# A two-layer attention kernel: where a half projection, a value piece, the first loads and the last denominators stand

## The chip, the cores and the metric

The kernel runs on one core of a Trainium2 chip. The metric is device time in microseconds (us). Before the change three runs took 3836.77, 3838.15 and 3838.79 us, so the median is 3838.15.

A core has a matrix engine (TensorE, PE in the profile; its weight loads are PEld), a vector engine (VectorE, DVE), an engine for functions such as exp (ScalarE, ACT), a general one (GpSimd, POOL) and SyncE (SP), which here only issues transfers (DMAs). TensorE writes its products to an accumulator memory, PSUM. Here PSUM is used as eight buffers of 128 x 512 floats, called banks.

## The reference

Sixteen images of 256 channels and 32 x 32 = 1024 positions pass through two layers, all in float32:

```python
# layer 0: 4 heads of 64
q, k, v = split(x @ w_proj + b_proj)             # per head
attn = softmax(q @ k.T * 64 ** -0.5)
x = (attn @ v) @ w_out + b_out + x
# layer 1: 8 heads of 32
g = group_norm(x)                                # 32 groups of 8 channels
q, k, v = split(g @ qkv_w.T)
attn = softmax(q @ k.T * 32 ** -0.5 + phys_bias) # one number per head
x = x + (attn @ v) @ proj_w.T + proj_b
h = group_norm(x)
x = x + gelu(h @ w1.T + b1) @ w2.T + b2          # 1024 hidden units
```

A softmax divides by the sum of its exponentials, the denominators below. A group norm needs mean and variance over all positions of a group, so it can start only when all of x is there.

## The kernel before, in words

**Layout.** Channels lie on the 128 partitions in two chunks (`CC = 2`), positions along the rows. Positions are handled in two halves of 512 (`NT = 2`, `TB = 512`); keys in eight blocks of 128 (`SB = 8`).

**PSUM.** `wide` (L218) gives one of three double buffers of two banks each, `s0` to `s2`, the least recently used first; a number in the set `kept` is passed over. `bank` (L224) gives one of two single banks, `b0` and `b1`. That makes all eight.

**Products by columns.** `product` (L243, the matmuls of L246) cuts a product into pieces of `cols[0]` columns: 32 inside the attentions, 128 elsewhere. A float32 matmul stands in the trace as two records.

**First attention** (`attention_a`, L289). It works through four items, a half of the positions and a chunk of two heads each, with eight key blocks per item. One step, called a unit here, multiplies the scores `s_a` (L303), lets ScalarE take their exponentials `e_a` (L311), and two units later multiplies them with v into `acc_a` (L324), while VectorE adds the exponentials up in `es_a` (L336). Even items gather in banks 0 and 1, odd ones in double buffer 2, which is in `kept` meanwhile and leaves it when the item ends (L343). Then ScalarE copies one half out (L340) and VectorE adds the other (L341).

**Denominators.** When both chunks of a half are done, `normalise` (L348) multiplies the sums with ones (`den_a`, L355). `denominators` (L258) writes the result to memory in another shape, inverts it there as 128 x 16 (L267), adds it to the totals `dsum` and `isum`, from which the kernel decides at its end whether all sums were in range, and reads it back spread over the partitions (L273). `scale` (L368) multiplies by it, and `project` calls `out_proj` (L520, tile `o`), whose result VectorE adds to x (L533) with statistics for the norm (L537).

**Second attention** (`attention_b`, L398). A unit takes two key blocks for four heads: scores `s_b` (L422) in banks 0 and 1 and all three double buffers, exponentials `e_b` (L437), sums `es_b` (L452), `acc_b` in bank 0 (L461), denominators `den_b` in bank 1 (L485), projection `j`.

**Norms.** `group_norm` (L540) averages over channel groups by two small matmuls (`gm`, `gv`) with short VectorE steps between, and writes the normed tile (L595) that the next products read.

**The order of work.** Functions are put off by counts of steps: `later.after(n, fn)` runs `fn` at the n-th following `tick`. `run` (L750) goes through an attention's units, runs the pieces that `fill` lists for a unit and ticks. Pieces are the projections for q, k and v (`qkv`, L603: pieces `qk` and `v`), and the two products of the MLP (`mlp`, L703: `hidden` at L709 and `outputs`, both tile `m`). Image b's second attention is filled with its own remaining `qk` and `v` pieces, image b-1's `outputs` and image b+1's first projections. The `hidden` pieces of b-1 stand between b's two attentions, while b's first norm is computed. The library's scheduler then orders each engine's instructions from this written order: it may issue ahead one that is ready sooner by its own estimate. `keep_in_program_order` pins one instruction behind the one written before it on its engine, not the later ones behind it. Engines meet through semaphores, and each engine runs its queue in order.

**The ends.** Weights `wp` are loaded on ScalarE's and GpSimd's queues (L92), biases on GpSimd's (L104 to L110), the other weights on ScalarE's (L125), x on SP's (L235). The exponential of `phys_bias` is taken at L157. In the last image four of the eight `outputs` pieces are kept back for the end (L821), where the last norm and the last MLP have nothing else beside them.

Of the kernel before, what the change touches and what calls it, by code (L numbers as in the profile page):

```python
# [54 lines left out]
def kernel(  # L55
# [44 lines left out]
    bp = b_proj.rearrange("(g i t d) -> i t d g", i=2, t=3, d=D0)  # L100
    bqk = const.tile([P, 3, HEADS0 // 2], F32, name="bqk")
    for i in range(2):
        for t in range(3):
            nc.gpsimd.dma_start(bqk[i * D0 : (i + 1) * D0, t, :], bp[i, t])  # L104
    pb = const.tile([P, HEADS1], F32, name="pb")
    nc.gpsimd.dma_start(pb, phys_bias.partition_broadcast(P))
# [15 lines left out]
    def load_mat(w, name):  # L122
        k, n = w.shape
        t = const.tile([P, k // P, n], F32, name=name)
        nc.scalar.dma_start(t, w.rearrange("(c p) n -> p c n", p=P))  # L125
        return t

    wo = load_mat(w_out, "wo")
# [5 lines left out]
    ident = const.tile([P, P], F32, name="ident")  # L134
    make_identity(nc, ident)
# [14 lines left out]
    mhalf = const.tile([P, CC], F32, name="mhalf")  # L150
    nc.gpsimd.memset(mhalf, -0.5)
    ones = const.tile([P, D0], F32, name="ones")
    nc.gpsimd.memset(ones, 1.0)
# [3 lines left out]
    nc.scalar.activation(ebias, pb, AF.Exp)  # L157
    eones = const.tile([P, HEADS1, D1], F32, name="eones")
    nc.vector.tensor_copy(eones, ebias.unsqueeze(2).to_broadcast([P, HEADS1, D1]))
# [4 lines left out]
    with ExitStack() as first:  # L164
        first_pass(
            first, tc, x, out,
            dict(
                wp=wp, bqk=bqk, pb=pb, bo=bo, g1w=g1w, g1b=g1b, g2w=g2w,
                g2b=g2b, pjb=pjb, m1b=m1b, m2b=m2b, wo=wo, wq=wq, wpj=wpj, w1=w1,
                w2=w2, ident=ident, gavg=gavg, mhalf=mhalf, ones=ones, eones=eones,  # L170
                bvo=bvo,
                in_range=in_range,
            ),
        )
# [14 lines left out]
def first_pass(ctx, tc, x, out, k):  # L189
# [23 lines left out]

    def use(n):
        order.remove(n)
        order.append(n)
# [10 lines left out]

    dsum, isum = (act.tile([P, 4 * TB // P], F32, name=n) for n in ("dsum", "isum"))
# [3 lines left out]
    def load_x(b):  # L232
        t = act.tile([P, CC, S], F32, tag="x", name=f"x_{b}", bufs=3)
        for cc in range(CC):
            nc.sync.dma_start(t[:, cc, :], x[b, cc * P : (cc + 1) * P, :])  # L235
        return t

# [51 lines left out]
    def attention_a(b, qT, kT, v, project):  # L289
# [24 lines left out]
        def weigh(i, kb, e):  # L314
            t, c = items[i]
            if kb == 0:
                if i % 2:
                    acc = wide(f"acc_{key}_{i}", 2)
                    accs[i] = [acc[:, h, :] for h in range(2)]
                else:  # L320
                    accs[i] = [bank(f"acc_{key}_{i}_{h}", h) for h in range(2)]
            for h in range(2):
                for g in range(2):
                    nc.tensor.matmul(  # L324
                        accs[i][h][g * D : (g + 1) * D, :],
                        v[h * HALF : (h + 1) * HALF, kb, c * 2 + g],
                        e[h * HALF : (h + 1) * HALF, g, :],
                        start=(kb == 0),
                        stop=(kb == SB - 1),
                    )  # L330
            if kb == 0:
                held[i] = e
                return
            if kb == 1:
                sums[i] = work.tile([P, 2, TB], F32, tag="es", name=f"es_{key}_{i}", bufs=4)
            nc.vector.tensor_add(sums[i], held[i] if kb == 1 else sums[i], e)  # L336
            if kb == SB - 1:
                r = res[:, c, t * TB : (t + 1) * TB]
                one, two = accs.pop(i)
                nc.scalar.copy(r, one)  # L340
                nc.vector.tensor_add(r, r, two)  # L341
                if i % 2:
                    kept.discard(2)  # L343
                if c == CC - 1:
                    later.after(1, lambda: normalise(t))
# [21 lines left out]

        def scale(t, full):  # L368
            r = res[:, :, t * TB : (t + 1) * TB]
            halves = [  # L370
                y.rearrange(form, c=CC, h=2)
                for y, form in ((r, "p c (h q) -> p c h q"), (full, "p (h c q) -> p c h q"))
            ]
            tc.keep_in_program_order(nc.vector.tensor_mul(halves[0], *halves))
            later.after(1 if t < NT - 1 else 4, lambda: project(t, res))
# [10 lines left out]
        while pending:  # L386
            weigh(*pending.pop(0))
            if not pending:
                cols[0] = P
            yield  # L390
# [7 lines left out]
    def attention_b(b, qT, kT, v, project):  # L398
# [82 lines left out]
        def normalise(i, r, last):  # L481
            t, c = items[i]
            den = bank(f"den_{key}_{i}", 1)
            for g in range(G):
# [6 lines left out]
                )  # L491
            denominators(
                f"{key}_{i}", den_copy(f"{key}_{i}", den), TB,
                ((3, 5) if b + 1 < B else (1, 1)) if last else (1, 1),
# [3 lines left out]
        def scale(i, r, last, full):  # L498
            t, c = items[i]
            tc.keep_in_program_order(nc.vector.tensor_mul(r, r, full))  # L500
            if c == CC - 1:
                wait = (10 if b + 1 < B else 1) if last else 1
                later.after(wait, lambda: project(t, res[t]))
# [16 lines left out]
    def out_proj(key, w, nk, src, bias, xs, t, stats):  # L520
        ps = wide(f"{key}_{t}")
        for co in range(CC):
            for kc in range(nk):
                product(
                    ps[:, co, :],
                    w[:, kc, co * P : (co + 1) * P],
                    src(kc),
                    start=(kc == 0),
                    stop=(kc == nk - 1),
                )  # L530
        for co in range(CC):
            y = xs[:, co, t * TB : (t + 1) * TB]
            nc.vector.scalar_tensor_tensor(  # L533
                y, ps[:, co, :], bias[:, co : co + 1], y, ALU.add, ALU.add
            )
            if stats is not None:
                nc.vector.bn_stats(stats[:, co, t, :], y)  # L537


    def group_norm(key, src, stats, gw, gb, tag, out_tile, wait):  # L540
# [25 lines left out]
        def variances():  # L566
# [3 lines left out]

            dv = small.tile([P, CC], F32, tag="dv", name=f"dv_{key}")
# [7 lines left out]
        def apply():  # L579
            rstd = small.tile([P, CC], F32, tag="rstd", name=f"rstd_{key}")  # L580
            for sl, ps in averages(f"gv_{key}", st["tv"]):
                nc.vector.tensor_scalar(rstd[sl], ps, EPS, None, ALU.add)
            nc.gpsimd.tensor_tensor(rstd, rstd, k["mhalf"], ALU.pow)
# [19 lines left out]
    def qkv(key, D, src, weights, b_qk, v_scale, qT, kT, v_dst):  # L603
        def qk(ch, which, t):
            ps = wide(f"qk_{key}_{ch}_{which}_{t}")[:, 0]
# [16 lines left out]
        def v(n):  # L622
            ps = wide(f"v_{key}_{n}")[:, 0]
# [47 lines left out]
    def attention_0(b, qkv_tiles, xb, norm):  # L671
# [3 lines left out]
        def project(t, res):  # L675
            out_proj(
                f"o{b}", k["wo"], CC,
                lambda kc: res[:, kc, t * TB : (t + 1) * TB],
                k["bvo"], xb, t, stats,
            )  # L680
            if t == NT - 1:
                norm(stats)
# [3 lines left out]
    def attention_1(b, qkv_tiles, xb, norm):  # L686
# [3 lines left out]
        def project(t, res):  # L690
            out_proj(
                f"j{b}", k["wpj"], CC,
                lambda kc: res[:, kc, :],
                k["pjb"], xb, t, stats,
            )
            if t == NT - 1:
                norm(stats)
# [70 lines left out]


    xs = {0: load_x(0)}  # L770
    tiles0, (first_qk, first_v) = qkv_0(0, xs[0])
    run_pieces(first_qk + first_v)

# [17 lines left out]
    for b in range(B):  # L791
# [20 lines left out]

        run_pieces(qk[:n] + v[:1])
        own = [v[1], qk[n], v[2], qk[n + 1], v[3], *qk[n + 2 :]]
# [4 lines left out]
        if b == B - 1:  # L819

            now, end = outputs[:4], outputs[4:]  # L821
# [9 lines left out]
        for m, pieces in enumerate(rest):  # L831
# [7 lines left out]
                    4 if b + 1 < B else 2,  # L839
# [308 lines left out]
```

## Time and profile before

| | us |
|---|---|
| median of 3 runs | 3838.15 |
| the profiled execution | 3836.97 |
| its span, first to last instruction | 3835.1 |
| outside the span | 1.9 |
| TensorE busy | 3783.2 |
| VectorE busy | 2214.2 |
| ScalarE busy | 2033.7 |

A line of a waits view names the waiting engine, tile and line, then what it waited for, the total in us, the number of times and the longest. A timeline line has the start and the time taken in us, engine, line, operation, output tile <- inputs, shape (for TensorE first rows * columns of the array, then the moving operand) and the count merged into it; in brackets the idle time before it and who ended it. Matmuls overlap: one that takes 0.59 us is followed by the next of its kind before it ends, so starts are compared, not ends. Times in all views run from the start of the span.

### The profile page before, as it was taken

To read this page: it belongs to the slowest core of one execution; us is meant where nothing else is said; L and a number is where in the kernel's file an instruction comes from. 1 tells how busy PE (TensorE), PEld (TensorE's weight loads), DVE (VectorE), ACT (ScalarE), POOL (GpSimd) and SP (SyncE) were. 2 spreads that over 40 slices of the span, in tenths; PEclk is the share of its full clock that TensorE was granted. 3 is DMA by queue.
4 is the path that set the end of the run, shared out by engine and by line. 5 is a ranking of instruction groups with operands and counts; after the bars stand their busy time and mean duration, and the time that the engine had idled before them with its cause. 6 is when DMAs were issued, how large, how long until landed. Compare 5 with 4: busy or idle time off the path is not lost.

```text
span 3835.1 us, 87391 instructions
## 1 busy us (share of the span) xinstructions
PE 3783.2 (99%) x38637; PEld 1508.9 (39%) x38637; DVE 2214.2 (58%) x2761; ACT 2033.7 (53%) x2625; POOL 86.1 (2%) x252
## 2 busy tenths in 40 slices
PE   9999999999999999999999999999999999999999
PEld 3333343333433334333343333433333333343435
DVE  4574646646466464665656556565564655646572
ACT  4555546555455554555545455554655546555461
POOL 1000000000000000000000000000000000000000
PEclk9999999999999999999999999999999999999999
DMA  2000000000000000010000001010000000000000
GB/s 83 10 16 12 30 12 16 27 13 30 12 16 28 11 30 12 19 29 7 30 12 27 21 10 32 7 32 15 13 30 7 32 15 13 29 7 24 12 14 23
DMA packets 62450, 78.58 MB, mean 20 GB/s; under 512 B 35344, under 2 KB 36880, under 8 KB 62064
## 3 DMA queue, kind: packets, MB, share of 16 engines
q1 hardware_dynamic: 57728, 68.72, 5.9%
q8 instruction: 304, 4.98, 0.5%
q10 hardware_dynamic: 3712, 3.80, 0.3%
q14 instruction: 82, 0.67, 0.1%
q0 software_dynamic: 624, 0.41, 0.1%
HBM read 54.54 MB, written 17.56 MB: 19 GB/s over the span
## 4 chain that ended last, share of the span: by engine, by line
PE 90%; DVE 5%; issue 2%; ACT 2%; DMA 1%; POOL 0%; SPq 0%; ACTq 0%; POOLq 0%; DVEq 0%
PE s_b L422 12%; PE m L709 12%; PE acc_b L461 12%; PE m L246 11%; PE s_a L303 10%; PE acc_a L324 9%; PE qk_b L246 6%; PE qk_a L246 6%; PE v_b L246 3%; PE j L246 3%; PE v_a L246 3%; DVE es_a L336 2%; PE o L246 2%; PE den_b L485 1%; ACT e_a L311 1%
## 5 line engine op out<-in xcount | busy, mean ns | idle before, releaser
L437 ACT ACTIVATE e_b<-s_b 128x1024 f32<-128x1024 f32 (+1 forms) x1280 | 982.7, 864 | 469.4 <-PE s_b L422 469.4
L452 DVE TENSOR_TENSOR es_b<-es_b,e_b 128x1024 f32<-128x1024 f32 x768 | 900.0, 1220 | 361.1 <-ACT e_b L437 361.1
L311 ACT ACTIVATE e_a<-s_a 128x1024 f32<-128x1024 f32 x512 | 521.4, 1025 | 450.1 <-PE s_a L303 438.3
L303 PE MATMUL s_a<-q,k 64*64 64x512 f32 x4096 | 562.1, 593 | 2.4 <-DVE x L533 2.4
L324 PE MATMUL acc_a<-e_a,v 64*64 64x512 f32 x4096 | 555.1, 589 | 0.0
L422 PE MATMUL s_b<-q,k 32*64 32x512 f32 x8192 | 536.3, 601 | 5.8 <-DVE res_b L477 4.9
L336 DVE TENSOR_TENSOR es_a<-es_a,e_a 128x1024 f32<-128x1024 f32 x384 | 469.0, 1221 | 111.5 <-ACT e_a L311 106.7
L461 PE MATMUL acc_b<-e_b,v 128*32 128x512 f32 x4096 | 492.1, 598 | 0.0
L709 PE MATMUL m<-gn_h,w 128*128 128x512 f32 x1024 | 460.8, 601 | 6.0 <-DVE mean_g L569 3.8
L246 PE MATMUL m<-g,w 128*32 128x256 f32 (+1 forms) x7616 | 464.0, 379 | 0.0
L246 PEld LDWEIGHTS m<-g,w 128*32 128x32 f32 (+1 forms) x7616 | 277.7, 112 | 215.8 <-issue 41.5
L717 ACT ACTIVATE g<-m,m1b 128x512 f32<-128x512 f32 x256 | 174.3, 687 | 342.7 <-PE m L709 342.5
L422 PEld LDWEIGHTS s_b<-q,k 32*64 32x64 f32 x8192 | 173.8, 130 | 294.0 <-issue 155.7
L324 PEld LDWEIGHTS acc_a<-e_a,v 64*64 64x64 f32 x4096 | 183.2, 133 | 260.9 <-issue 224.9
L709 PEld LDWEIGHTS m<-gn_h,w 128*128 128x128 f32 x1024 | 189.3, 191 | 244.9 <-issue 227.9
L303 PEld LDWEIGHTS s_a<-q,k 64*64 64x64 f32 x4096 | 167.3, 133 | 280.6 <-issue 199.2
L461 PEld LDWEIGHTS acc_b<-e_b,v 128*32 128x32 f32 x4096 | 108.5, 109 | 351.6 <-ACT e_b L437 194.7
L477 DVE TENSOR_TENSOR res_b<-res_b,acc_b 128x512 f32<-128x512 f32 x192 | 131.1, 683 | 190.9 <-PE acc_b L461 190.9
L246 PE MATMUL qk_a<-x,wp 128*32 128x512 f32 (+1 forms) x1856 | 234.1, 594 | 7.2 <-DMA wp<-in_L_conv_w_proj_dram 5.9
L246 PE MATMUL qk_b<-gn_g,wq 128*32 128x512 f32 (+1 forms) x1280 | 234.0, 592 | 0.0
L452 DVE TENSOR_TENSOR es_b<-e_b,e_b 128x1024 f32<-128x1024 f32 x128 | 150.8, 1219 | 52.4 <-ACT e_b L437 52.4
L639 DVE TENSOR_TENSOR v<-v_b,eones 128x512 f32<-128x512 f32 x64 | 43.9, 686 | 227.8 <-PE v_b L246 227.8
(112 smaller groups left out, 2070.1 us busy)
## 6 DMA issues: line engine op xcount, KB each, us to landing
x<-in_x_dram SPq DMA_DIRECT2D x32, 512.0 KB
rd_a<-row_a SPq DMA_DIRECT2D x64, 256.0 KB
rd_b<-row_b SPq DMA_DIRECT2D x256, 64.0 KB
out_dram<-x SPq DMA_DIRECT2D x64, 256.0 KB
w<-in_L_conv_mlp_w_dram ACTq DMA_DIRECT2D x2, 1024.0 KB
sp_b<-d_b SPq DMA_DIRECT2D x64, 8.0 KB
row_b<-inv_b SPq DMA_DIRECT2D x64, 8.0 KB
wq<-in_L_conv_qkv_w_dram ACTq DMA_DIRECT2D x1, 768.0 KB
```

The lines of the kernel that those rows point to most:

```text
L246: nc.tensor.matmul(o[sl], w[:, sl], r, **flags)
L303: nc.tensor.matmul(s[h : h + HALF, g, :], kT[g * D : (g + 1) * D, c, kb * P + h : kb * P + h + HALF], qT[g * D : (g + 1) * D, c, t * TB : ...
L311: nc.scalar.activation(e, s, AF.Exp, scale=float(D) ** -0.5)
L324: nc.tensor.matmul(accs[i][h][g * D : (g + 1) * D, :], v[h * HALF : (h + 1) * HALF, kb, c * 2 + g], e[h * HALF : (h + 1) * HALF, g, :], st ...
L336: nc.vector.tensor_add(sums[i], held[i] if kb == 1 else sums[i], e)
L422: nc.tensor.matmul(outs[g][h : h + HALF, :], kT[g * D : (g + 1) * D, c, k0 : k0 + HALF], qT[g * D : (g + 1) * D, c, t * TB : (t + 1) * TB] ...
L437: nc.scalar.activation(to, s, AF.Exp, scale=float(D) ** -0.5)
L452: ins = nc.vector.tensor_add(d, es[n] if kb == 0 else d, es[2 * block + n])
L461: nc.tensor.matmul(acc[g * D : (g + 1) * D, :], v[:, kb + m, c * G + g], es[2 * m + g // 2][:, g % 2, :], start=(m == 0), stop=(m == 1),)
L477: nc.vector.tensor_add(r, r, acc)
L709: nc.tensor.matmul(ps, k["w1"][:, cc, hc * P : (hc + 1) * P], hn[0][:, cc, t * TB : (t + 1) * TB], start=(cc == 0), stop=(cc == CC - 1),)
L717: nc.scalar.activation(g, ps, AF.Gelu, bias=k["m1b"][:, hc : hc + 1])
```

## The change

- **First layer's half projection.** `out_proj` becomes a function that returns `issue`, which may do one output chunk at a time, and outside the attentions uses banks 0 and 1 instead of a double buffer. The projection of half 0 is no longer put off behind its scaling; it is done in two parts at the end of `attention_a`, one before and one after the tick that writes the second half's denominators. Double buffer 2 leaves `kept` two ticks after an odd item, and half 0's denominators are written after two ticks instead of one.
- **Second layer's last projection of an image** (`handed`) is no longer put off by ten ticks but written right behind the next image's first denominators.
- **Second attention's first piece.** The first `v` piece inside `attention_b` takes bank 0 (`aside`, `single`) instead of a double buffer.
- **Fillers.** In the first and the last image the own pieces are spread over five units, and the `outputs` pieces, five in the last image, stand in every second unit after them. Three are kept back for the end.
- **Loads.** The first image is loaded in halves, and all loads of `bqk`, `phys_bias` and the other weights go to SP's queue behind it. The constants on GpSimd move ahead of its bias loads. The exponential of `phys_bias` follows the first projections. Three products of a zero tile (128 x 512) are written first.
- **Last denominators.** The last item of the last image inverts its denominators as 128 x 512 in VectorE straight from PSUM, with two reductions for the totals. In its norm 4 and 10 products of the 128 x 128 identity are written behind the two small matmuls.

```diff
+    def load_rest():
+        bp = b_proj.rearrange("(g i t d) -> i t d g", i=2, t=3, d=D0)
+        for t in (1, 0):
+            for i in range(2):
+                nc.sync.dma_start(bqk[i * D0 : (i + 1) * D0, t, :], bp[i, t])
+        nc.sync.dma_start(pb, phys_bias.partition_broadcast(P))
+        for i in range(2):
+            nc.sync.dma_start(bqk[i * D0 : (i + 1) * D0, 2, :], bp[i, 2])
+        for t, w in weights:
+            nc.sync.dma_start(t, w)
...
+    def single(name):
+        return bank(name, aside.pop()) if aside else wide(name)[:, 0, :]
...
     def load_x(b):
-        for cc in range(CC):
-            nc.sync.dma_start(t[:, cc, :], x[b, cc * P : (cc + 1) * P, :])
+        n = S if b else TB
+        for s0 in range(0, S, n):
+            for cc in range(CC):
+                nc.sync.dma_start(
+                    t[:, cc, s0 : s0 + n], x[b, cc * P : (cc + 1) * P, s0 : s0 + n]
+                )
...
+    def keep_warm(what, n):
+        ps = bank("warm", 1)
+        for _ in range(n):
+            nc.tensor.matmul(
+                ps[:, : what.shape[1]], what[:, :P], what, start=True, stop=True
+            )
...
                 if i % 2:
-                    kept.discard(2)
+                    later.after(2, lambda: kept.discard(2))
                 if c == CC - 1:
-                    later.after(1, lambda: normalise(t))
+                    later.after(2 if t < NT - 1 else 1, lambda: normalise(t))
...
+            if t == 0 and handed:
+                handed.pop()()
...
-            later.after(1 if t < NT - 1 else 4, lambda: project(t, res))
+            if t == NT - 1:
+                later.after(4, lambda: project(t, res)())
...
                 cols[0] = P
+                first_half = project(0, res)
+                first_half((0,))
+                yield
+                first_half((1,))
+                break
             yield
...
+            at_end = last and b == B - 1
...
+            if at_end:
+                full = work.tile([P, CC * TB], F32, tag="full", name="rd_end", bufs=1)
+                nc.vector.reciprocal(full[:, :TB], den)
+                scale(i, r, last, full[:, :TB])
+                for tot, what in ((dsum, den), (isum, full[:, :TB])):
+                    part = small.tile([P, 1], F32, tag="part", name="part")
+                    nc.vector.tensor_reduce(part, what, AX.X, ALU.add)
+                    nc.gpsimd.tensor_add(tot[:, :1], tot[:, :1], part)
+                return
...
-                wait = (10 if b + 1 < B else 1) if last else 1
-                later.after(wait, lambda: project(t, res[t]))
+                issue = project(t, res[t])
+                if last and b + 1 < B:
+                    handed.append(issue)
+                else:
+                    later.after(1, issue)
...
+    def out_proj(key, w, src, bias, xs, t, stats, then):
+        todo = list(range(CC))
+
+        def issue(cos=range(CC)):
+            apart = cols[0] == P
+            if not apart:
+                both = wide(f"{key}_{t}")
...
+            for co in cos:
+                ps[co] = bank(f"{key}_{t}_{co}", co) if apart else both[:, co, :]
...
+            if not todo and then:
+                then()
+
+        return issue
...
+            if at_end:
+                keep_warm(k["ident"], 4)
...
+            if at_end:
+                keep_warm(k["ident"], 10)
...
+    nothing = work.tile([P, TB], F32, tag="d", name="nothing", bufs=1)
+    nc.vector.memset(nothing, 0.0)
+    keep_warm(nothing, 3)
     xs = {0: load_x(0)}
+    k["load_rest"]()
     tiles0, (first_qk, first_v) = qkv_0(0, xs[0])
     run_pieces(first_qk + first_v)
+    k["exp_bias"]()
...
+        def early(piece):
+            aside.append(0)
+            piece()
+
+        own = [lambda: early(v[1]), qk[n], v[2], qk[n + 1], v[3], *qk[n + 2 :]]
...
-            now, end = outputs[:4], outputs[4:]
+            now, end = outputs[:5], outputs[5:]
+        if not first:
+            fill = {0: own[:2], 1: own[2:3], 2: own[3:5], 3: own[5:6], 4: own[6:]}
+            fill.update({5 + 2 * m: [piece] for m, piece in enumerate(now)})
+            now = []
```

## The prediction

> **What bounds the kernel now.** I read the page's shares first, then who TensorE waited for, then TensorE's own timeline through one batch, then both ends of the span.
>
> ```profile
> PE 3783.2 (99%) x38637; PEld 1508.9 (39%) x38637; DVE 2214.2 (58%) x2761; ACT 2033.7 (53%) x2625; POOL 86.1 (2%) x252
> PEclk9999999999999999999999999999999999999999
> ```
>
> TensorE is the bound: busy 99%, at full clock in every slice, with VectorE and ScalarE near half. Only time in which TensorE stands still, or multiplies at less than its rate, can be won; the change removes no product. The waits, TensorE's alone:
>
> ```profile
> PE v_b L246 <- ACT e_b L437: 19.2, 16, 1.2
> ...
> PE m L709 <- DVE mean_g L569: 3.8, 15, 0.3
> PE j L246 <- DVE res_a L341: 3.1, 15, 0.2
> PE s_a L303 <- DVE x L533: 2.4, 15, 0.2
> ```
>
> Four waits come once a batch. They look small (some 28 us) because a modelled matmul end covers part of a stall. The spacing of the starts tells the true loss. TensorE's timeline of one steady batch:
>
> ```profile
> 253.04 1.04 PE L324 MATMUL acc_a<-e_a,v 64*64 64x512 f32 x8
> 254.01 1.07 PE L355 MATMUL den_a<-es_a,ones 128*32 128x256 f32 x16
> 255.01 1.07 PE L303 MATMUL s_a<-q,k 64*64 64x512 f32 x2
> 256.28 3.64 PE L246 MATMUL j<-res_b,wpj 128*32 128x512 f32 x32 [0.21 <-DVE res_a L341]
> ...
> 273.98 3.64 PE L246 MATMUL o<-res_a,wo 128*32 128x512 f32 x32
> 277.55 1.09 PE L303 MATMUL s_a<-q,k 64*64 64x512 f32 x8
> 278.45 1.04 PE L324 MATMUL acc_a<-e_a,v 64*64 64x512 f32 x8
> 279.65 1.09 PE L303 MATMUL s_a<-q,k 64*64 64x512 f32 x8 [0.16 <-DVE x L533]
> ...
> 331.92 1.97 PE L422 MATMUL s_b<-q,k 32*64 32x512 f32 x32
> 335.09 1.93 PE L246 MATMUL v_b<-wq,gn_g 128*32 128x256 f32 x32 [1.20 <-ACT e_b L437]
> ...
> 338.67 1.97 PE L422 MATMUL s_b<-q,k 32*64 32x512 f32 x32
> 340.57 1.92 PE L461 MATMUL acc_b<-e_b,v 128*32 128x512 f32 x16
> ```
>
> Undisturbed, a group of 8 s_a or acc_a starts 0.86 after the one before, s_b takes 1.90 and acc_b 1.74; what exceeds these is lost.
>
> **Part by part**, against the profiled execution's own 3836.97 us.
>
> **A, v in bank 0.** From s_b to v_b it is 3.17 us, against 1.90 from s_b to acc_b: 1.27 lost, 16 times, 20.3 us. v_b waits for a double buffer that ScalarE frees after two exponentials of 128x512 (594 ns each) and one of 128x1024 (1043 ns). Bank 0 is free after the first. ScalarE starts at 333.04, so v_b can start near 333.7, where s_b's products end. The next piece, qk_b, then comes near 335.5 and its double buffer is free at 335.0. New: the second unit's scores write bank 0, near 337.3, and VectorE must have copied v out of it (686 ns). v is complete near 335.8; the sums es_b (1.22 each) become ready at 335.99 and 337.13. If v goes first it is out by 336.5 and nothing waits. Behind both sums it is out at 338.96, as today, and those scores start 0.3 later than today's 338.67: -5 us in all. The scores for the other buffers can be put ahead. Ends -5 and 20.3; I take 1.1 each, **17.6**.
>
> **B, the accumulator's buffer kept two ticks, denominators one unit later, j behind them.** After 255.01 two s_a matmuls need 0.21, so j could start at 255.23, and starts at 256.28: 1.05 lost. j has taken the double buffer with the accumulators just finished, and VectorE empties it only at 256.24. Afterwards the denominators take that buffer one unit (1.72) later, near 255.6, and j takes another. The denominators can still wait 0.6 unless j is put ahead, so 0.4 to 1.05; I take 0.9 in 15 batches, 13.5, and 1.5 for the first batch, where the denominators wait 1.4 in the same way. **15.0** (6 to 17.5). The norm behind j moves by a unit; its output is used at 290.12, while it is ready near 276.
>
> **C, the half projection o moved.** Now: 0.22 before o (acc_a's last group starts at 272.90, so o could at 273.76), 0.14 in it (3.57 against the 3.43 of the undivided one at 305.15), 0.04, and 0.34 at the wait for x. That is 0.74 in 16 batches, 11.8. At its new place the switch from 64 to 128 rows is paid already by the matmul that stands there. Its two additions (0.745 each) and statistics (0.68 each) move with it to where VectorE is idle. What could be late is the norm: half of it (1.72) now follows the denominators. But the first quarter of gn_g is ready near 316.5, qk_b first reads it at 323.23, and other matmuls fill between: 6.7 us of cover. **11.5** (5 to 11.8).
>
> **D, the norm's small products.** gm_g to the next m is 0.53, gv_g to m 0.14: 0.39 lost, 15 times, 5.9. The second o no longer takes a double buffer, which may free m or not: 0 to 5.9. **2.**
>
> **E, fillers spread in the first and last batch.** Scores in the last batch start at 3702.88, 3707.52, 3712.12, 3717.12, 3722.37 and 3728.99. Work is 3.64 a unit, 0.86 more with denominators, so unfilled units lose 0.1, 0.9, 1.3, 1.5, 2.1 and so on: 9.5 over the last eight. A filled unit loses next to nothing (3680.83 to 3688.04 is 7.21, its work). With a piece in every second unit only first-of-a-row losses stay, about 0.9 three times and some 1 more: 5.5 won (2 to 7). In the first batch 11 units stay bare where 12 were: 0.5. **6.0.**
>
> **F, the end.** The m pieces of the last batch but one run out near 3767.2:
>
> ```profile
> 3768.28 0.38 PE L246 MATMUL gm_h<-mean_c_h,gavg 128*128 128x2 f32 x2 [0.80 <-DVE mean_c_h L562]
> 3769.50 0.38 PE L246 MATMUL gv_h<-tv_h,gavg 128*128 128x2 f32 x2 [0.84 <-DVE tv_h L575]
> 3772.08 2.93 PE L709 MATMUL m<-gn_h,w 128*128 128x512 f32 x3 [2.20 <-DVE gn_h L595]
> ```
>
> Between 3772.1 and 3777.2 the granted clock is 0.52 in the table by stretches: after that gap six matmuls start 0.855 apart instead of 0.43, 2.6 us. The denominators' trip through memory (3749.99 to 3760.93) gives way to a reciprocal of 128x512, of which there is no row. The 128x16 one takes 0.247 where a reduction of as many elements takes 0.171: some 5 ns an element, 2.7 us. The Trainium skill (VectorE: DVE Perf Modes, "First, the fixed hardware budget") says the divider repeats eight times; eight times the pass implied by 1.22 us for 1024 elements is an estimate of 4.9. With 0.69 for the scaling and 0.25 between engines that is 3.6 or 5.8. Cover: one m piece (3.43) and those half products of j that need no scaling (two of 0.86). By the row nothing waits, by the rule 0.7. I take the row, as it is the same instruction. Then j's additions, statistics and means (2.0) lie under the two pieces left (6.9), so gm_h's 0.8 and 0.3 around it go; the 3.8 from gm_h to m stay. They are filled by 14 idle products (0.21 each, 3.0), which hold the clock. If gm_h is put among the pieces, those 3.0 are the price. **3.7** (1.1 if the clock falls anyway; 7.5). The six transfers of that trip go, and two reductions (0.6 each by the rows of 512) lie under j's 3.43.
>
> **G, the start.** The eight first pieces take from 5.93 to 24.29, 18.4 us; at full clock 13.7. Lost: 3.1 in the slow clock until near 12, 1.2 in the wait for k's copy, rest small. That copy waited at 14.88 because ScalarE's queue was issuing weights until 13.16. These go to SP behind x and bqk, so its queue is free near 3. bqk, sixth on SP at 0.4 to 0.5 each and 6.8 from issue to landing by the POOL rows, is there near 10; the fourth piece needs it at 11.1. Behind it on SP wait wo (used at 33.2) and the second x (used near 95): both covered, as 7.4 MB landed in 25 us. The three warm-up products take 5.1 us at the slow clock. The skill (TensorE: Matmul & The Clock Gate, "What's actually happening") asks for one full busy window of about 3.4 us that starts where it likes, so up to 6.8; the trace needed 6.1 at the start, 4.9 at the end. By the row about 1 us stays slow, costing 0.5; by the rule at worst 1.7, costing 0.85. A second table load (1.28) before the first exponential may cost 0.5. **3.5** (0 to 5).
>
> **H, new small waits** at the moved steps: the two pieces left without the third buffer for a unit, moved table and sums: **-4** (0 to -10), a guess within the switch costs above (0.15 each, one or two a batch).
>
> Sum 17.6 + 15.0 + 11.5 + 2 + 6.0 + 3.7 + 3.5 - 4 = 55.3. So 3836.97 - 55.3 = 3781.7; the median of the runs lies 1.2 above the profiled one: **3783**. All good ends together give 3762.
>
> **Rivals.** *v is emptied late*: A is nothing, 3800.6; for it, es_b stand earlier in the written order and become ready within 0.3 us of v; against it, v's data come first. *Waits move*: A half, B and C a third of theirs, E and F half: about 22 us won, 3816. For it, the denominators now depend on the buffer that j waited for; against it, VectorE is half idle. *Nothing comes of it*, 3838: that needs all of A, B and C to return, though each has its own cause. *Slower*: the norm chain. If the moved half and its VectorE work made gn_g later than its 6.7 us of cover, each us beyond costs 16. It eats the 55 at 3.5 beyond, a delay of 10.2; at 11.5 the time is 3858. Against it: I count 1.72 and 2.85 of added work, 4.6 at most.
>
> **Chances.** Forecast 0.54 (own range 3766 to 3795), late v 0.24, waits move 0.13, nothing 0.05, slower 0.04. A difference of 0.2% (7.7 us) is what can be told: faster 0.91, same 0.05, slower 0.04. Leaving out the last two cases and the edges, 3767 to 3814 should hold it 8 times in 10.
>
> **What would show it.** A: the wait of v_b for e_b gone and v_b 1.9 after s_b; wrong if s_b then waits for v. B: no j or den_a wait for res_a. C: no o between s_a groups, o with x8 twice at the end, qk_b without wait. E: last batch's scores at even distances. F: clock full to the end, m after gv_h with half the gap. G: v_a near 20.3. The forecast falls if waits for es_b, v or gn_g take a microsecond a batch.

## The result, and the profile after

The changed kernel takes **3809.55 us** (median of four runs, 3809.28 to 3809.72), beside 3837.46 for the kernel before on the same chip (3836.66 to 3838.79). The ratio is **0.9927**, with a 95% interval of 0.991 to 0.9944: 27.9 us faster where the forecast had 55. That is outside the forecast's own range, 3766 to 3795, and inside the wider one, 3767 to 3814.

The page's shares and clock of the changed kernel:

```profile
PE 3757.8 (99%) x38335; PEld 1490.8 (39%) x38335; DVE 2230.3 (59%) x2764; ACT 2034.1 (53%) x2624; POOL 79.0 (2%) x245
...
PEclk9999999999999999999999999999999999999999
```

TensorE is still the bound, 99% busy at full clock. Its waits (who waits, for whom; total us, times, longest):

```profile
PE s_b L467 <- DVE v L721: 24.6, 16, 1.5
PE den_a L389 <- DVE res_a L374: 8.1, 16, 0.8
PE s_b L467 <- DVE res_b L522: 4.4, 8, 0.9
PE s_a L336 <- ACT e_a L344: 3.3, 15, 0.2
...
PE qk_a L279 <- DMA x<-in_x_dram: 1.0, 1, 1.0
PE m L787 <- DVE gn_h L677: 0.3, 1, 0.3
PE j L279 <- DVE part L545: 0.2, 1, 0.2
```

The waits that the change aimed at are gone: v_b for e_b, m for mean_g, j for res_a, s_a for x. The first line is new and is longer than the one that it replaces: the scores wait for **v**, 1.5 us in each of 16 batches, where v_b had waited 1.2. TensorE's timeline shows both the half projection o in its new place and the new wait (start, time taken, engine, line, output <- inputs, array, moving operand, count):

```profile
250.59 1.04 PE L357 MATMUL acc_a<-e_a,v 64*64 64x512 f32 x8
252.11 1.07 PE L389 MATMUL den_a<-es_a,ones 128*32 128x256 f32 x16 [0.49 <-DVE res_a L374]
253.00 3.62 PE L279 MATMUL j<-res_b,wpj 128*32 128x512 f32 x32
...
281.37 1.98 PE L279 MATMUL o<-res_a,wo 128*128 128x512 f32 x4
283.29 1.07 PE L389 MATMUL den_a<-es_a,ones 128*32 128x256 f32 x16
284.29 1.98 PE L279 MATMUL o<-res_a,wo 128*128 128x512 f32 x4
...
326.14 1.97 PE L467 MATMUL s_b<-q,k 32*64 32x512 f32 x32
328.05 1.93 PE L279 MATMUL v_b<-wq,gn_g 128*32 128x256 f32 x32
329.80 1.90 PE L279 MATMUL qk_b<-gn_g,wq 128*32 128x512 f32 x16
333.23 1.98 PE L467 MATMUL s_b<-q,k 32*64 32x512 f32 x32 [1.53 <-DVE v L721]
```

v_b now starts 1.91 us after s_b, as foretold (it was 3.17). The unit is none the shorter: from its s_b to the next unit's s_b it is 7.09, where it was 6.76. j follows the denominators without a gap, but the denominators themselves start 1.52 after acc_a, where 0.97 was usual.

Cut at such starts, the two profiled executions (spans 3835.10 and 3807.84) can be laid side by side, in us over the whole run. In the last batch five outputs pieces stand in the attention where there were four, so one piece is taken off on either side:

| stretch | before | after | difference | forecast |
|---|---|---|---|---|
| up to the first s_a | 31.3 | 28.3 | -3.0 | G: -3.5 |
| first s_a to first qk_b (first attention and hidden pieces), 16 batches | 1568.0 | 1542.0 | -26.0 | B, C, D, H: -24.5 |
| first unit of the second attention, 16 times | 108.1 | 113.4 | +5.3 | A: -17.6 |
| first batch from the second unit on | 88.4 | 89.1 | +0.7 | E: -0.5 |
| last batch, second unit to last den_b; after without its fifth outputs piece (3.43) | 96.1 | 94.2 | -1.9 | E: -5.5 |
| last den_b to the end; before without its fourth kept piece (3.43) | 82.8 | 80.4 | -2.4 | F: -3.7 |

The stretches not listed are the same to a tenth; these rows make 27.3. A alone accounts for 22.9 of the 28 that are missing, E for another 4.8.

### The profile page after: what moved, and what is told of

It is laid out like the page before. It is cut to its first block, busy times and chain, and to the rows that moved or that the text cites. A ratio compares the mean times of both kernels' runs of the same rounds, so it can differ in the third digit from the quotient of the medians.

```text
span 3807.8 us, 86808 instructions
## 1 busy us (share of the span) xinstructions
PE 3757.8 (99%) x38335; PEld 1490.8 (39%) x38335; DVE 2230.3 (59%) x2764; ACT 2034.1 (53%) x2624; POOL 79.0 (2%) x245
## 4 chain that ended last, share of the span: by engine, by line
PE 94%; DVE 2%; ACT 2%; issue 2%; DMA 0%; ACTq 0%; POOLq 0%; POOL 0%; DVEq 0%
PE s_b L467 13%; PE acc_b L506 12%; PE m L787 12%; PE m L279 12%; PE s_a L336 11%; PE acc_a L357 10%; PE qk_a L279 6%; PE qk_b L279 5%; PE o L279 3%; PE v_a L279 3%; PE j L279 3%; PE v_b L279 2%; PE den_b L531 1%; ACT e_b L482 1%; DVE es_b L497 1%
## 5 line engine op out<-in xcount | busy, mean ns | idle before, releaser
L482 ACT ACTIVATE e_b<-s_b 128x1024 f32<-128x1024 f32 (+1 forms) x1280 | 982.6, 865 | 500.0 <-PE s_b L467 500.0
L336 PE MATMUL s_a<-q,k 64*64 64x512 f32 x4096 | 530.9, 592 | 3.3 <-ACT e_a L344 3.3
L357 PE MATMUL acc_a<-e_a,v 64*64 64x512 f32 x4096 | 527.6, 589 | 0.0
L787 PE MATMUL m<-gn_h,w 128*128 128x512 f32 x1024 | 451.3, 595 | 0.3 <-DVE gn_h L677 0.3
L357 PEld LDWEIGHTS acc_a<-e_a,v 64*64 64x64 f32 x4096 | 160.1, 133 | 279.3 <-issue 242.4
L336 PEld LDWEIGHTS s_a<-q,k 64*64 64x64 f32 x4096 | 153.1, 133 | 276.8 <-issue 216.2
```

Of the source, the lines that this page charges most:

```text
L336: nc.tensor.matmul(s[h : h + HALF, g, :], kT[g * D : (g + 1) * D, c, kb * P + h : kb * P + h + HALF], qT[g * D : (g + 1) * D, c, t * TB : ...
L357: nc.tensor.matmul(accs[i][h][g * D : (g + 1) * D, :], v[h * HALF : (h + 1) * HALF, kb, c * 2 + g], e[h * HALF : (h + 1) * HALF, g, :], st ...
L482: nc.scalar.activation(to, s, AF.Exp, scale=float(D) ** -0.5)
L787: nc.tensor.matmul(ps, k["w1"][:, cc, hc * P : (hc + 1) * P], hn[0][:, cc, t * TB : (t + 1) * TB], start=(cc == 0), stop=(cc == CC - 1),)
```

## The experiments

They start from the changed kernel, unless the text says otherwise. The kernel before took 3837.15, 3837.93 and 3837.43 us beside the three groups of runs. Each ratio is to that.

**1. v ahead of the sums.** On VectorE the copy of v was written behind the unit's two sums es_b. Here the piece is written first.

```diff
             add(*now, 0)
+            if u == units[0]:
+                ahead()              # early(v[1])
             if pending:
...
-        own = [lambda: early(v[1]), qk[n], ...
+        own = [lambda: None, qk[n], ...
```

> After, with the one v piece written ahead of the first unit's two sums, so that VectorE copies v out of bank 0 first. Theory 'order': the 1.5 us that the second unit's scores wait for v, 16 times, is the time v stands behind the two sums (1.22 each); it goes, unit 0 falls from 7.09 to about 5.5 us and the time by 25.6 us, to 3784. Rival 'bank': bank 0 is in use too soon again whatever the order, or ScalarE's exponentials become the limit; the wait gets another name, unit 0 stays near 7 and the time within 5 us of 3809.5. With v first the two sums must not delay anything else.

Measured: **3784.23** (3783.85 to 3784.42), ratio 0.9861 (0.9844 to 0.9877). VectorE in that unit, first the changed kernel:

```profile
330.21 2.36 DVE L497 TENSOR_TENSOR es_b<-e_b,e_b 128x1024 f32<-128x1024 f32 x2 [3.27 <-ACT e_b L482]
332.49 0.68 DVE L721 TENSOR_TENSOR v<-v_b,eones 128x512 f32<-128x512 f32 x1
```

then this variant, which reaches the same point 1.2 us earlier in the run:

```profile
328.84 0.69 DVE L723 TENSOR_TENSOR v<-v_b,eones 128x512 f32<-128x512 f32 x1 [3.10 <-PE v_b L279]
329.45 2.35 DVE L497 TENSOR_TENSOR es_b<-e_b,e_b 128x1024 f32<-128x1024 f32 x2
```

In the changed kernel v_b's products have all started by 329.8, VectorE is idle until 330.21, and then takes both sums first. v goes out at 332.49, and the scores that reuse bank 0 start at 333.23. With v first, the unit takes 5.48 instead of 7.09; 16 times 1.61 is 25.8 us, and the median fell by 25.3. The start is 0.4 longer, all other stretches are the same to a tenth. This variant is the fastest of all that ran, and the next ones start from it where the text says so.

**2. The double buffer back for v, and 3. bank 0 alone, in the kernel before** (there with `single` and `early` added).

```diff
-        own = [lambda: early(v[1]), qk[n], ...     # 2, in the kernel after
+        own = [v[1], qk[n], ...
...
-        own = [v[1], qk[n], ...                    # 3, in the kernel before
+        own = [lambda: early(v[1]), qk[n], ...
```

> After, with this v piece back in a double buffer. Theory 'order': the single bank cost more than it won, 0.33 us a batch by the traces (7.09 against 6.76 for unit 0), so this is about 5 us faster than the change as made, 3804. Rival 'bank helps': the single bank won something that the traces of the two kernels hide; slower than 3809.5.

> The kernel before with nothing but the v piece in bank 0. Theory 'order': the loss does not need the rest of the change: unit 0 goes from 6.76 to 7.09, 5 us slower than before, 3843. The forecast's step A taken alone would give 3820. If it comes out faster than before, the wait for v comes from another part of the change.

Measured: 3804.49 (ratio 0.9914, 0.9897 to 0.993) and 3844.1 (ratio 1.0018, 1.001 to 1.0026). The waits of the second of these, beside its first unit at 7.09:

```profile
PE s_b L427 <- DVE v L644: 24.6, 16, 1.5
```

By the starts, the 16 first units are 5.3 us longer with bank 0 in either kernel (the medians differ by 5.1 and 7.0), so nothing else in the change has a hand in it. Together with experiment 1 this shows that the loss is VectorE's order.

**4. The half projection back in the first attention**, one tick behind its scaling, with B left in.

```diff
-            if t == NT - 1:
-                later.after(4, lambda: project(t, res)())
+            later.after(1 if t < NT - 1 else 4, lambda: project(t, res)())
...
-                first_half = project(0, res)
-                first_half((0,))
-                yield
-                first_half((1,))
-                break
```

> After, with the first layer's half projection back behind its scaling, inside the attention. Theory: the move of the half projection by itself is worth 0.8 us a batch (switches of the array's shape 0.4, the wait for x 0.35), so 12 to 13 us slower than after, 3822. Rival: the 1.6 us a batch won in this stage come from the denominators and j alone; then within 4 us of 3809.5.

Measured: **3869.77**, ratio 1.0081 (1.0064 to 1.0098), 48 us above the expectation. TensorE at the new wait:

```profile
272.96 1.04 PE L357 MATMUL acc_a<-e_a,v 64*64 64x512 f32 x8
276.94 3.64 PE L279 MATMUL o<-res_a,wo 128*32 128x512 f32 x32 [2.94 <-DVE res_a L411]
```

and what VectorE does in that time:

```profile
271.89 1.92 DVE L671 TENSOR_SCALAR gn_h<-x,ga_h,gc_h 128x512 f32<-128x512 f32 x4
273.72 1.22 DVE L369 TENSOR_TENSOR es_a<-e_a,e_a 128x1024 f32<-128x1024 f32 x1
274.97 0.69 DVE L374 TENSOR_TENSOR res_a<-res_a,acc_a 128x512 f32<-128x512 f32 x1
275.58 1.22 DVE L411 TENSOR_TENSOR res_a<-res_a,rd_a 128x1024 f32<-128x1024 f32 x1
```

B writes the denominators a unit later. That puts the scaling (L411) behind the norm's four steps, a sum and an addition, 3.7 us of queue. o stands where it stood, so it waits 2.94 in every steady batch. The first attention and the hidden stage together grow by 60.4 us over the 16 batches, which is the whole difference to the changed kernel. Not all of it is the wait: in six of the 16 batches the granted clock falls to 0.50 around the start of o, for 3.4 us in four of them and 6.8 in two. These batches are 1.4 to 2.9 us longer than the others, 12.0 together. Parts B and C can't be added up as two gains: with B, o has to stand further behind.

**5. The half projection three ticks behind its scaling**, in the variant with v first. The diff is those of experiments 1 and 4, with 3 for 1.

> The v-first kernel, with the half projection inside the attention again, but three ticks after its scaling, so that the scaling is surely done. Theory: what is left of the 65 us that its return cost is the switches of the array's shape and the wait for x, 0.8 us a batch: 12 to 14 us slower than v-first, 3797. Rival: the projection needs its old place for another reason (VectorE's queue); then still 30 us or more slower.

Measured: 3785.86, ratio 0.9865 (0.9848 to 0.9881), 1.6 us above the variant, not 13. o there starts 0.97 after acc_a and the scores follow it without a wait. Beyond o's own 3.43, which has changed its stretch, a batch loses 0.10 us by the starts (0.30 more in the attention, 0.20 less in the hidden stage). So once o stands far enough behind its scaling, the move into the norm's gap is worth next to nothing.

**6. The same three ticks in the kernel before.**

```diff
-            later.after(1 if t < NT - 1 else 4, lambda: project(t, res))
+            later.after(3 if t < NT - 1 else 4, lambda: project(t, res))
```

> The kernel before with one number changed: the half projection o follows its scaling by three units instead of one, and stays in the first attention. Theory 'VectorE's queue': o's loss of 0.78 us a batch is mostly the two additions of o queueing on VectorE behind the norm's four steps (gn_h) and the accumulator's addition; two units later the queue is empty, so 0.4 to 0.7 a batch is won, 6 to 11 us: 3829 (3827 to 3831). Rival 'the place itself' (a product of another tile shape between scores costs it wherever it stands, as the forecast's part C had it): no change, 3837.

Measured: 3832.31, ratio 0.9986 (0.9979 to 0.9993). The first attention takes 64.54 a batch instead of 64.93, so 0.39, just below the expected 0.4 to 0.7; the median fell by 5.1 us, short of the expected 6 to 11. TensorE and VectorE behind o:

```profile
281.12 3.64 PE L246 MATMUL o<-res_a,wo 128*32 128x512 f32 x32
284.69 1.09 PE L303 MATMUL s_a<-q,k 64*64 64x512 f32 x8
285.60 1.04 PE L324 MATMUL acc_a<-e_a,v 64*64 64x512 f32 x8
286.45 1.04 PE L303 MATMUL s_a<-q,k 64*64 64x512 f32 x8
```

```profile
284.82 1.41 DVE L533 SCALAR_TENSOR_TENSOR x<-o,bvo,x 128x512 f32<-128x512 f32 x2 [0.47 <-PE o L246]
```

The scores that stood 1.20 behind acc_a in the kernel before (278.45 to 279.65, with 0.16 of it shown as a wait for x) are now 0.85 behind. VectorE is idle when o ends, where before it was still at gn_h, a sum and an addition. The queue took that part of o's loss. The 0.22 ahead of o stays.

**7. Denominators another unit later**, in the variant with v first.

```diff
-                    later.after(2 if t < NT - 1 else 1, lambda: normalise(t))
+                    later.after(3 if t < NT - 1 else 1, lambda: normalise(t))
```

> The v-first kernel (3784.2), with the first half's denominators after three ticks instead of two. Theory: they wait 0.5 to 0.8 us a batch (8.2 in all) because the accumulator's buffer that they take is emptied 0.6 us after their turn; one unit (1.72 us) more covers that, so 9 us faster, 3775, and the wait den_a for res_a is gone. Rival: the wait only moves to j, to the norm behind it or to the half projection; within 3 us of 3784.

Measured: **3815.52**, ratio 0.9942 (0.9926 to 0.9959), 31 us worse than the variant instead of 9 better. Its waits:

```profile
PE v_b L279 <- ACT e_b L482: 17.1, 15, 1.1
PE s_a L336 <- DVE res_a L374: 8.1, 16, 0.8
...
PE s_a L336 <- ACT e_a L344: 4.2, 15, 0.3
PE s_a L336 <- DVE rstd_h L664: 3.8, 15, 0.3
```

The 8.1 for res_a is the same to a tenth, under another name. With the accumulators in the third double buffer, whoever comes next for a buffer waits for VectorE's addition: the denominators, or the scores when these go ahead. This wait wasn't escaped by a swap of those who queue for the buffer. The first line is another matter. The group of ScalarE's table loads at L482 (count, busy us, mean ns, idle before them and what ended it) is, in the variant with v first,

```profile
L482 ACT ACT_TABLE_LOAD x15 | 19.2, 1283 | 0.3
```

and here:

```profile
L482 ACT ACT_TABLE_LOAD x15 | 19.2, 1283 | 33.0 <-PE s_b L467 33.0
```

The load of the exponential's table, 1.28 us, was made while ScalarE had nothing to do ahead of the batch's first exponential. Here it is made after the wait for the scores, on the path. In the variant the first exponential of a batch carries the wait for TensorE's count itself. Here that wait is an instruction of its own and stands ahead of the load: in the batch whose s_b starts at 326.10 it ends at 327.24, the load starts at 327.26 and the exponential at 328.56. What made the compiler choose differently was not settled. By the starts, 15 of the 16 first units take 6.69 instead of 5.48, 18.1 in all, and the first attentions are 13.3 longer; together 31.4. The 13.3 are 0.88 in each of 15 batches: 0.16 around the denominators, 0.24 ahead of gv_h, and 0.48 behind it, where the scores now wait for rstd_h.

**8. The second norm's averages one unit sooner, and 9. two units sooner**, in the variant with v first.

```diff
-                    4 if b + 1 < B else 2, b == B - 1,
+                    3 if b + 1 < B else 2, b == B - 1,      # 9: 2
```

> The v-first kernel, with the second norm's averages three ticks behind j's statistics instead of four. Theory: j moved by one unit has pushed gv_h past the start of an odd item, where double buffer 2 is kept and only two are left, so the scores behind gv_h wait for the exponential of the scores just before (0.46 us lost a batch, 15 times). A tick sooner it stands in the even item again: 7 us faster, 3777, and no wait of s_a for e_a. Rival: gv_h costs that wherever it stands, or its means are not ready a tick sooner; within 2 us of 3784 or slower.

> This is the variant with v ahead of the sums (3784.2 us), with the first norm's averages two units sooner after the new statistics instead of four. Theory 'third buffer': the small product gv_h costs the scores behind it 0.46 us a batch only because it then stands where an accumulator holds the third double buffer; one unit sooner, where it still stood ahead of that accumulator's first scores, changed nothing, two units sooner puts it among scores that turn over three buffers. So gv_h to s_a falls from 0.46 to below 0.1, 15 times, some 6 us: 3778. Rival 'price of the small product': the 0.46 belongs to gv_h itself wherever it stands: 3784.

(The second expectation says "first norm"; its edit is to the second, like the other's.) Measured: 3784.18, no change, and **3794.98** (ratio 0.9889, 0.9873 to 0.9906), 10.8 worse. Of the second:

```profile
PE gm_h L632 <- DVE mean_c_h L642: 9.5, 15, 0.6
```

Two units sooner the first small product stands ahead of its data. The averages' inputs come at 259.33 and gm_h starts at 259.48, after 0.64 of waiting, with the scores queued behind it. The other one, gv_h, costs 0.32 there instead of 0.46: the next scores start 1.17 after their acc_a instead of 0.86. So the third buffer was a small part of it at most. A product of two columns still holds a double buffer until VectorE has read it: gv_h starts at 263.05, VectorE reads it at 264.75 behind a sum of 1.23, and the delayed scores start at 265.14.

**10. The idle products left out**, in the variant with v first. They enter no output.

```diff
-            if at_end:
-                keep_warm(k["ident"], 4)
...
-            if at_end:
-                keep_warm(k["ident"], 10)
```

> The v-first kernel without the 14 identity products in the last norm. Theory: they hold the clock (2.6 us) and stretch the way from gm_h to the first m by 0.5 us, so without them 2 us slower, 3786, with the clock at half for some 5 us after the gap. Rival: the shorter gap alone keeps the clock up; then 0.5 us faster.

Measured: 3786.2 (ratio 0.9865, 0.9849 to 0.9882), 2.0 slower (2.8 in the last stretch, against 0.8 at the start, which differs between executions). From gm_h to m it is 4.03 us instead of 4.36, but the granted clock falls to 0.50 for the 6.8 us from 3720.3 on, where the variant keeps 1.00. The 14 products pay, though m starts later with them.

**11. Two pieces in the second unit** of the first and the last batch, in the variant with v first.

```diff
-            fill = {0: own[:2], 1: own[2:3], 2: own[3:5], 3: own[5:6], 4: own[6:]}
+            fill = {0: own[:2], 1: own[2:4], 2: own[4:5], 3: own[5:6], 4: own[6:]}
```

> The variant with v ahead of the sums, with two pieces (v2 and one of qk) in the second unit of the second attention of the first and the last batch, and one each in the third and fourth. Theory: that unit lost 1.2 us in each of the two batches because only the v piece was left in it, so 2.4 us: 3781.8. Rival: the loss moves to the third unit, which then has one piece less: 3784.

Measured: 3785.11 (ratio 0.9864, 0.9848 to 0.9881), 0.9 slower. The loss moves with the lone v piece, and grows. TensorE in the third and fourth unit of the first batch:

```profile
140.48 1.91 PE L279 MATMUL v_b<-wq,gn_g 128*32 128x256 f32 x32
142.32 1.95 PE L467 MATMUL s_b<-q,k 32*64 32x512 f32 x24
144.96 1.09 PE L467 MATMUL s_b<-q,k 32*64 32x512 f32 x8 [0.69 <-DVE v L723]
```

The scores take 3.66 to the next group instead of 1.90. It is experiment 1 over again: they come right behind v_b, need the buffer that v leaves, and v's copy stands behind VectorE's sums. A qk piece, which ScalarE copies out, would have covered it.

**12. Everything together**: v first, averages two units sooner, second unit filled, first image loaded whole. On top of the edits of experiments 1, 9 and 11:

```diff
-        n = S if b else TB
+        n = S
```

> All that should help together: v ahead of the sums, the norm's averages two units sooner, the second unit filled, and the first image loaded whole (one transfer ahead of the others in place of two halves, the wait for the second half was 0.4 to 1.1 us). If the gains add, 3784.2 - 6 - 2.4 - 0.5 = 3775.3; if the third-buffer theory falls, 3781.

Measured: 3795.56, ratio 0.9891 (0.9874 to 0.9907): 3784.23 plus the 10.8 and 0.9 of its two bad parts less a small gain at the start. The first s_a starts at 27.7, where ten executions of the changed kernel and its other variants lie between 27.9 and 29.3. That is too near to their spread to call it a gain.

## Why the forecast was off, step by step

The rival *v is emptied late* came true, and worse than it was put: A is not nothing but a loss of 5.3. With A at -5.3 and E at 1.2 the forecast's own sum would have been 3810.7, 1.2 above the measured median.

**A failed, at its bad end.** The forecast took 1.1 us won each; 0.33 was lost, 5.3 in all, and the low end had been -5. It had the condition right ("behind both sums ... those scores start 0.3 later"), and named it again as the rival *v is emptied late*. What failed is the argument against that rival: "v's data come first". They did, by a fraction of a microsecond, and VectorE was idle then; but the two sums, written first, also ran first. Experiment 1 shows the cause, and the forecast's 17.6 as within reach: written first, the unit is 1.28 shorter than in the kernel before, 20.5 in all.

**B, C, D and H came out right in sum, 26.0 for 24.5, and part of that is luck.** D won about 4.5 us more than was taken and H lost 2.8 more. Per steady batch, from the starts of the groups:

- B: 0.81 won (forecast 0.9). j's gap of 1.05 is gone, and the denominators start 0.55 later behind acc_a than they did, inside the 0.6 that the forecast allowed. That no such wait for res_a would be left was to show B; it is there, and experiment 7 shows that it belongs to the buffer.
- C: 0.81 won (forecast 0.72). The forecast counted 0.40 for switches of the array's shape and the like, and 0.34 for the wait for x. Experiment 6 bears out the second: 0.39 comes from VectorE's queue behind o. Experiment 5 speaks against the first: 0.10 is all that the new place adds once o is far enough behind its scaling. The other 0.3 lies between these two kernels. By the starts, o begins 0.97 behind acc_a in experiment 5, not 1.08, and its denominators stand ahead of the first m, which makes the hidden stage 0.2 shorter. C without B was not run; experiment 4 shows that with B in, o had to move or lose 2.94 a batch.
- D: 0.43 won, all of it, where 2 of 5.9 us had been taken. m follows gm_g after 0.14 (304.99 to 305.13). In experiment 5 it does so too, though the first o is not in the gap there, so that move isn't what frees m. The forecast's own reason, that the second o no longer takes a double buffer, fits both kernels and was not tested alone.
- H: gv_h costs 0.45 more (6.8 in all, against 4 guessed). TensorE around it, before and after:

```profile
269.35 1.14 PE L324 MATMUL acc_a<-e_a,v 64*64 64x512 f32 x8
...
271.19 1.14 PE L324 MATMUL acc_a<-e_a,v 64*64 64x512 f32 x8
```

```profile
266.10 1.10 PE L357 MATMUL acc_a<-e_a,v 64*64 64x512 f32 x8
267.01 0.24 PE L630 MATMUL gv_h<-tv_h,gavg 64*64 64x2 f32 x4
267.48 1.09 PE L336 MATMUL s_a<-q,k 64*64 64x512 f32 x8 [0.22 <-ACT e_a L344]
268.39 1.04 PE L357 MATMUL acc_a<-e_a,v 64*64 64x512 f32 x8
```

From one acc_a to the next it is 2.29 where it was 1.84. j a unit later has moved the norm's second average with it, and the scores behind it now wait for ScalarE's exponential. Experiments 8 and 9 found no better place for it.

**E was mis-sized: 1.2 instead of 6.0.** The step that failed is "with a piece in every second unit only first-of-a-row losses stay". That was to leave 3.7 us. By the starts, the last batch's eleven units from the sixth on lost 10.9 before (10.0 of it in the last eight, where the forecast read 9.5) and lose 7.9 after:

```profile
3666.49 1.07 PE L467 MATMUL s_b<-q,k 32*64 32x512 f32 x2
3667.98 1.97 PE L467 MATMUL s_b<-q,k 32*64 32x512 f32 x30 [0.43 <-DVE res_b L522]
...
3680.14 2.72 PE L467 MATMUL s_b<-q,k 32*64 32x512 f32 x32
...
3691.85 1.07 PE L467 MATMUL s_b<-q,k 32*64 32x512 f32 x2
```

A filled unit and the bare one behind it take 13.65 (3666.49 to 3680.14) and 11.71 (3680.14 to 3691.85) by turns, where their work is 11.57 and 10.71. The trace names a wait of 0.43 for VectorE's res_b in three of the eleven; the cause of the rest stays open, and no run tested this part. Another 1.2 is lost in the third unit of both batches, behind a lone v piece (experiment 11). To a tenth, that leaves the 1.9 won in the last batch, and in the first it makes the loss of 0.7.

**F was mis-sized: 2.4 instead of 3.7.** The reciprocal of 128x512 took

```profile
L541 DVE RECIPROCAL rd_end<-den_b 128x512 f32<-128x512 f32 x1 | 3.3, 3347 | 0.0
```

3.35 us, between the row's estimate of 2.7 and the estimate of 4.9 worked out from the Trainium skill (VectorE: DVE Perf Modes, "First, the fixed hardware budget"). By the rule j would have waited 0.7; it waited 0.24. The end of the last norm:

```profile
3742.84 0.28 PE L279 MATMUL gm_h<-mean_c_h,gavg 128*128 128x2 f32 x2
...
3744.87 2.03 PE L267 MATMUL warm<-ident 128*128 128x128 f32 x16
3747.20 13.14 PE L787 MATMUL m<-gn_h,w 128*128 128x512 f32 x30 [0.30 <-DVE gn_h L677]
```

From gm_h to m it is 4.36 us, where it was 3.80 and was to stay so: 0.56 lost, of which the idle products account for 0.33 (4.03 without them, experiment 10). From gv_h to m it is 2.47, where it was 2.58, and not the half that was to show F. In exchange the clock stays full (1.00 from 3747 to 3753, where before it was 0.52 from 3772.1 to 3777.2), which gives 2.4 from m to the end, and of the 1.1 counted at gm_h 0.6 goes. Without the products the clock falls and the run is 2.0 slower (experiment 10), so the clock is what they buy.

**G was right: 3.0 instead of 3.5.** v_a starts at 21.32 (forecast 20.3), 2.97 sooner than before. The clock is full from 5.16, after 3.7 us of products; before it was from 12.06, after 6.1. That early clock is in part luck. Over the fourteen profiled executions the full clock comes between 3.3 and 6.1 us after TensorE's first product, and the eleven that start with the idle products alone span nearly all of that (3.3 in experiment 9, 6.1 in experiment 2). This fits, but for a tenth at the lower end, the forecast's reading of the Trainium skill (TensorE: Matmul & The Clock Gate, "What's actually happening"), where a window of about 3.4 us runs freely: an estimate of 3.4 to 6.8. The rest is eaten by a wait for the second half of x, which is now a transfer of its own (1.0 here, between nothing and 1.2 in the variants), and by ScalarE: its first table load, 1.28 us, and k's copy behind it start only when bqk has landed, at 10.60 and 11.89. Executions of the changed kernel and its variants differ by up to 1.3 in that stretch, so a few tenths in G mean little.

## What to carry to other kernels

When a buffer is freed sooner, look for the instruction that empties it and read its engine's queue in order: here data that were ready first left first only when that was written first. Before a step is moved, list what its engine holds between the step and its reader; here such queues on VectorE, 59% busy, made A's loss, half of o's, the 2.94 of experiment 4 and the loss at the lone v piece. The wait on the last free buffer changed its name and not its length (8.1 us) when those who queue for it were swapped.

## What was unexpected of the hardware

A table load of 1283 ns on ScalarE lay hidden 15 times in one program and on the path 15 times in another that differs only in one delay count (experiment 7): 17.1 us of waits. In experiment 4, where TensorE waits 2.94 us once a batch, the granted clock fell to 0.50 around six of the 16 waits and stayed at 1.00 in the ten other batches. Behind the same idle products it was full after 3.3 us in one execution and after 6.1 in another. VectorE's reciprocal took 6.5 ns an element on a row of 512 from PSUM (3347 ns), and 15.4 on a row of 16 (246 ns), so a line through the two gives 6.25 ns an element and, as an estimate, 146 ns of fixed part; the forecast's estimate from the short row was 0.65 us low.
